# Output projection with channels on partitions, slice logits from its sum, and a gather in two column tiles: a two-layer fused kernel on one Trainium2 core

## The chip, the cores and the metric

The kernel runs on one core of one Trainium2 chip. The metric is the device time of one execution in microseconds (us). A core has five engines that run side by side: TensorE (PE, with its weight loads shown as PEld), VectorE (DVE), ScalarE (ACT), GpSimd (POOL) and SyncE (SP), which here only issues DMAs. They meet at semaphores: an instruction waits until another engine has counted far enough, and everything behind it on its own engine waits with it.

## The reference, cut to what matters

The input is one image of 256 channels and 48 x 48 = 2304 positions ("tokens"). All arithmetic is in fp32.

```python
# layer 0: group norm, attention over all (token, head) pairs, output projection, residual
xt = transpose(group_norm(x))
q, k, v = xt @ Wq.T + bq, xt @ Wk.T + bk, xt @ Wv.T + bv      # 4 heads of 64
A = softmax(qf @ kf.T / 8, axis=1)                            # 9216 x 9216
x = x + (A @ vf).reshape(...) @ Wo.T + bo
# layer 1, attention: tokens are soft-assigned to 64 slices
t = tokens(x); n = layer_norm(t)
h = n @ W0 + b0
sw = softmax(h @ Ws + bs)                                     # 2304 x 64
# q, k, v of the slices: (h @ Wqkv + bqkv) summed over tokens with weights sw,
# divided by the sum of sw; attention among the slices; back to tokens by sw; @ Wout + bout
t = t + slice_attention(...)
# layer 1, experts: top 2 of 8 gates, each expert 256 -> 1024 -> 256 with gelu
t = t + sum of w_e * expert_e(layer_norm(t))
```

## The kernel before

**Stages.** Projections of layer 0; the attention of layer 0; a tail that finishes the last two token tiles; slice attention; gating and routing; the experts. A second copy of the layers for extreme inputs is behind a branch that is not taken.

**Layout.** Tokens are cut into 18 tiles (`NTT`) of 128. `x_sb` holds x with channels on partitions, `[128, 2, 2304]`; `t_sb` holds it with tokens on partitions, 256 channels and 8 columns for gates.

**Projections.** Queries and keys come first, in token blocks; then 18 tiles of values go through the V loop: two matmuls (line 330) into one of five PSUM banks and a VectorE addition into `v_sb` (line 334). Behind it, before the attention, stand fourteen small matmuls (lines 347 to 365) that fold `W0 @ Ws` into the slice weights `Wl` and `Wout @ Wg` into gate columns of `Wout_sb`, with column sums `cs_bc` of the gate weights, by which a mean is taken off later.

**Attention.** The 9216 queries are taken in 18 blocks (`b`), each against 36 pairs of key tiles. A pair is four 64x64-tile matmuls of scores `s`, one exponential `p` on ScalarE over 1024 columns, four matmuls `av` of values, and one VectorE addition into `acc`. `s` has two buffers, `p` five, `av` one. Two blocks make one group `g` of 256 tokens; the normalized result goes to `OT[:, g % 2]`.

**Work between pairs.** In pair 0 of a block, `close` finishes the block before: `both` (the sum of the two halves of `acc`), `partition_all_reduce` of it into `total` on POOL, and `up`, which reads `av`. In pair 1, `between(b - 1)` puts the side work of earlier token tiles on PE, ahead of the first `av` of the block; its VectorE and ScalarE parts go into a list `later`, of which one item is taken per pair, in the order of the ranks that stand beside them. Pieces of side work, each for one token tile `i`:

- `out_proj`: two transposes of `x_sb` and two matmuls with `WoT` in one bank, whose sum is x plus projection with tokens on partitions; `add` puts `bo_bc` to it in `t_sb`, `spread` takes mean and variance and has POOL compute `rstd_t` by a power, `norm` writes `tn`;
- `turn`: two transposes of `tn`, copied to `tnT` by ScalarE;
- `slices`: two matmuls `tnT` x `Wl`; softmax to `sw`, and gate columns of `t_sb`, for which the scale is undone;
- `gather`: two matmuls of 64 columns, `tn` x `sw`, added into `ts_sum`; `sw` is added into `sw_sum`.

`follow(k)` starts `out_proj` of tile k - 2, `turn` of k - 3, `slices` of k - 4 and `gather` of k - 5, two PSUM banks `pa` and `pb` among them:

```python
for lag, (step, ps) in enumerate(
    ((out_proj, pa), (turn, pa), (slices, pb), (gather, pb))
):
    if 0 <= k - 2 - lag < NTT - 2:
        work.extend(step(k - 2 - lag, ps))
```

In the last block, when `later` is empty, `follow` is called up to four more times, so that tiles 0 to 15 are done by its end.

**Order.** `pe`, `dve`, `act` and `pool` are wrappers that keep the program's order; what is issued through `nc.` may be moved by the scheduler (the projections, `nc.vector` constants). DMAs of SP keep their order.

**Tail.** Tiles 16 and 17 need the last two blocks. `out_proj`, `turn` and `slices` run for both, with eight transposes of `sw` and filler matmuls (`busy`, which keep PE occupied) between; then `pts` and `den` take their sums, `ph` is the first matmul of the slice attention. The memory of layer 0 is freed there, and SP loads the expert weights `w2_sb` (8 MB) and `b2_bc` into it.

## Time and profile before

| | us |
|---|---|
| median of 3 runs (lowest to highest) | 1604.61 (1604.38 to 1605.35) |
| the profiled execution, whole | 1603.17 |
| its span, first to last instruction | 1601.5 |
| PE, DVE, ACT, POOL busy in the span | 1571.7, 1059.7, 834.7, 193.2 |
| first score matmul of the attention at | 67.71 |
| last `av` of the attention from | 1224.64 |
| first `ph` of the slice attention at | 1241.68 |
| mean granted TensorE clock | 0.998 |

The profile lists for each engine what ran when. A line of the timeline has the start, the busy time, the engine, the source line (line 60 is that of the wrapper), the operation, `out<-in` by the names of the program, and the number of records merged; in brackets the idle time of the engine before it and what ended that. An fp32 matmul leaves two records, a transpose one. The ends of matmuls are modelled, so their starts are the better measure. The page also has shares by 40 slices, DMA queues, and the chain of work that ended last; that chain goes back only to 1303.9 us, inside the experts, so the attention is read from the timeline.

### The profile page before, as it was taken

Reading aid. Unit: us, or ns where it says so; the run is one execution under the profiler, and the core shown is the slowest. Engines: PE = TensorE matmul, PEld = TensorE weight load, DVE = VectorE, ACT = ScalarE, POOL = GpSimd, SP = SyncE. Lnnn points to the kernel's source line nnn. Section 1 sums busy time; section 2 is a strip of 40 time slices with the busy share of each in tenths; the row PEclk is TensorE's granted clock in tenths of the full one; section 3 lists DMA queues with packets and bytes.
Section 4 is the critical chain, followed back from the end, with each engine's and each line's share of the span. In section 5 each row is a group of like instructions: output and inputs, shape, how many; then the busy total and the mean of one; then the engine's idle time right before and its main releaser. Section 6 shows DMA issues by size and latency. Waiting matters only on the chain. (4 is left out here: it accounts for less than half of the span.)

```text
span 1601.5 us, 32032 instructions
## 1 busy us (share of the span) xinstructions
PE 1571.7 (98%) x13225; PEld 789.6 (49%) x13225; DVE 1059.7 (66%) x1379; ACT 834.7 (52%) x1178; POOL 193.2 (12%) x141
## 2 busy tenths in 40 slices
PE   7999999999999999999999999999999999999997
PEld 3633333333333333333333333333334689999996
DVE  6578788787787877878878778788787721111111
ACT  2266666565665656656656566566564533333331
POOL 0000001011010010110100101101000123433331
PEclk9999999999999999999999999999999999999999
DMA  4000000000000000000000000000001956666664
GB/s 138 1 1 1 1 1 1 1 1 1 1 1 1 2 1 2 1 1 2 1 1 1 1 1 1 1 1 1 1 2 55 300 162 188 180 183 182 181 186 143
DMA packets 38200, 77.58 MB, mean 48 GB/s; under 512 B 3565, under 2 KB 24378, under 8 KB 37914
## 3 DMA queue, kind: packets, MB, share of 16 engines
q1 hardware_dynamic: 30154, 64.78, 12.0%
q0 software_dynamic: 7344, 10.10, 3.7%
q8 instruction: 109, 1.79, 0.5%
q10 hardware_dynamic: 544, 0.52, 0.1%
q14 instruction: 49, 0.40, 0.1%
HBM read 63.07 MB, written 12.32 MB: 47 GB/s over the span
## 5 line engine op out<-in xcount | busy, mean ns | idle before, releaser
L60 ACT ACTIVATE p<-s 128x1024 f32<-128x1024 f32 x648 | 663.8, 1024 | 475.4 <-PE s L60 466.6
L60 DVE TENSOR_TENSOR acc<-acc,p 128x1024 f32<-128x1024 f32 x612 | 748.2, 1222 | 227.5 <-ACT p L60 216.8
L60 PE MATMUL av<-p,v_sb 64*64 64x512 f32 x5184 | 675.7, 590 | 2.1 <-DVE up L60 1.8
L60 PE MATMUL s<-q,kk 64*64 64x512 f32 x5184 | 675.4, 590 | 0.0
L60 PEld LDWEIGHTS s<-q,kk 64*64 64x64 f32 x5184 | 200.9, 133 | 353.2 <-issue 181.3
L60 PEld LDWEIGHTS av<-p,v_sb 64*64 64x64 f32 x5184 | 195.6, 131 | 355.9 <-ACT p L60 200.4
L60 ACT ACTIVATE hid<-ph,bcol 128x128 f32<-128x128 f32 x312 | 89.4, 368 | 200.8 <-PE ph L60 200.1
L60 POOL PARTITION_ALL_REDUCE total<-both x17 | 55.3, 3250 | 962.0 <-DVE both L60 962.0
L60 PE MATMUL py<-w_sb,hid 128*128 x624 | 146.9, 379 | 0.0
L60 PEld LDWEIGHTS ph<-xT,w 128*128 128x128 f32 x1248 | 145.3, 192 | 2.7 <-issue 0.8
L60 PE MATMUL ph<-xT,w 128*128 128x128 f32 x1248 | 145.7, 275 | 0.6 <-issue 0.6
L60 DVE COPY xT<-pt 128x256 f32<-128x256 f32 x39 | 16.5, 424 | 161.0 <-PE pt L60 161.0
L60 PEld LDWEIGHTS py<-w_sb,hid 128*128 128x128 f32 x624 | 112.8, 190 | 12.3
L1133 POOL DMA_INDIRECT t_d<-y,slot_t x38 | 60.1, 1582 | 163.9 <-DVE y L60 146.0
L60 DVE TENSOR_TENSOR y<-py,b_bc 128x256 f32<-128x256 f32 x39 | 16.6, 425 | 77.5 <-PE py L60 77.5
L60 POOL TENSOR_TENSOR rstd_t<-ve,mhalf 128x1 f32<-128x1 f32 (+3 forms) x22 | 28.0, 1273 | 205.2 <-DVE ve L60 205.2
L60 DVE TENSOR_TENSOR acc<-p 128x1024 f32<-128x1024 f32 x18 | 36.4, 2024 | 9.3 <-ACT p L60 9.3
L1133 POOL DMA_INDIRECT xs<-tn_d,slot_t x36 | 38.9, 1080 | 15.8 <-issue 9.9
L60 DVE RECIPROCAL rinv<-rinv 128x256 f32<-128x256 f32 x17 | 29.7, 1746 | 0.0
L318 DVE TENSOR_SCALAR q<-pp,bcol 64x512 f32<-64x512 f32 (+1 forms) x30 | 20.8, 694 | 8.0 <-PE pp L301 7.7
L60 DVE TENSOR_REDUCE up<-av 128x512 f32<-128x1024 f32 x18 | 21.9, 1216 | 0.0
L60 PE MATMUL spin<-Wqkv_sb,ident 128*128 128x256 f32 x90 | 20.9, 381 | 0.0
(292 smaller groups left out, 644.5 us busy)
## 6 DMA issues: line engine op xcount, KB each, us to landing
w<-in_L_ffn_W_dram SPq DMA_DIRECT2D x39, 1024.0 KB, 5.8
w_sb<-in_L_ffn_W_dram SPq DMA_DIRECT2D x8, 1024.0 KB, 11.9
x_sb<-in_x_dram SPq DMA_DIRECT2D x3, 576.0 KB
t_d<-t_sb SPq DMA_DIRECT2D x2, 768.0 KB, 5.4
tn_d<-tn SPq DMA_DIRECT2D x2, 768.0 KB
t_sb<-t_d SPq DMA_DIRECT2D x3, 512.0 KB, 6.2
out_dram<-ob SPq DMA_DIRECT2D x3, 512.0 KB
b_bc<-in_L_ffn_b_dram SPq DMA_DIRECT2D x1, 1024.0 KB
```

The lines of the kernel that those rows point to most:

```text
L60: return self.tc.keep_in_program_order(getattr(self.engine, name)(*args, **kwargs))
L318: nc.vector.tensor_scalar(dst, pq[rows, 0:tn], bcol[rows, B_Q + m : B_Q + m + 1], 0.125, ALU.add, ALU.mult,)
L1133: new = nc.gpsimd.indirect_dma_start(**kwargs)
```

## The change

The side work now goes by groups of two token tiles. `out_proj` computes Wo x O with channels on partitions (four matmuls of 256 columns) and adds it and `bo`, now a column of `bcol`, into `x_sb`. `slices` transposes `x_sb` into one bank for mean, variance and `t_sb`, and multiplies `x_sb` itself with `Wl`, whose columns have had their mean over the 256 channels taken off, so that the mean of a token falls out; the logits are scaled by `rstd_t` afterwards. `turn` and `tnT` are gone, and gate columns need no correction. `gather` has the two tiles of a group in the two column halves of PE: `sw` is the stationary operand (64 columns), `tn` with a column of ones (257) the moving one, and the sums of the halves and of `sw` stay in `sums_of` until the tail folds them with `fold`. `follow` does `out_proj` for even k, `gather` and `slices` for odd k. The last block has two extra calls, not four. In `close`, `up` is taken ahead of `both`. The small matmuls of the weights go into the V loop at tiles 3, 6 and 9. Routing has two operations fewer. The tail does its two tiles as one group.

```diff
-    sw_sum = const.tile([P, S], FP, name="sw_sum")
+    sums_of = const.tile([P, C + 1], FP, name="sums_of")
+    nc.vector.memset(ts_sum[:, 2 * S : 3 * S], 0.0)
+    fold = const.tile([P, 2, S], FP, name="fold")
+    fold_den = const.tile([P, S], FP, name="fold_den")
+    nc.vector.tensor_tensor(fold[:, 1, :], ident[:, 0:S], ident[:, S : 2 * S], ALU.add)
+    nc.vector.tensor_copy(fold[:, 0, :], fold[:, 1, :])
...
+    B_Q, B_K, B_0, B_QK, B_OUT, B_O = 64, 66, 68, 70, 74, 76
...
+        for r, (b, n) in {64: (bq, 2), 66: (bk, 2), 68: (b0, 2), 70: (bqkv, 4), 74: (bout, 2), 76: (bo, 2)}.items():
...
-    bo_bc = load_bcast(bo, C, "bo_bc")
...
+        def slice_weights():
+
+            pw = ps_w.tile([P, 512], FP, name="pw", tag="pw")
+            nc.vector.tensor_copy(Wl[:, :, S : S + E], Wg_sb)
+            for k, b in enumerate((B_0, B_0 + 1, B_OUT, B_OUT + 1)):
+                nc.vector.tensor_copy(brep[:, k, :], bcol[:, b : b + 1].to_broadcast([P, P]))
+            for ci in range(2):
+                for k in range(2):
+                    nc.tensor.matmul(
+                        pw[:, ci * S : (ci + 1) * S], W0T[:, k, ci * P : (ci + 1) * P], Ws_sb[:, k, :],
+                        start=(k == 0), stop=(k == 1),
+                    )
+            for k in range(2):
+                nc.tensor.matmul(
+                    pw[:, 128:192], brep[:, k, :], Ws_sb[:, k, :], start=(k == 0), stop=(k == 1)
+                )
+            nc.vector.tensor_copy(Wl[:, :, 0:S], pw[:, 0:128].rearrange("p (c s) -> p c s", c=2))
+            nc.vector.tensor_tensor(bl_bc, pw[:, 128:192], bs_bc, ALU.add)
+
+        def centred():
+
+            pw = ps_w.tile([P, 512], FP, name="pw", tag="pw")
+            for k in range(2):
+                nc.tensor.matmul(
+                    pw[:, 0 : S + E], ones, Wl[:, k, :], start=(k == 0), stop=(k == 1)
+                )
+            nc.vector.scalar_tensor_tensor(
+                Wl, pw[:, 0 : S + E].unsqueeze(1).to_broadcast([P, 2, S + E]), -1.0 / C, Wl,
+                ALU.mult, ALU.add,
+            )
...
+            elif i == 3:
+                slice_weights()
+            elif i == 6:
+                centred()
+            elif i == 9:
+                gate_weights()
...
+    tn = side.tile([P, 4, C + 1], FP, name="tn")
+    dve.memset(tn[:, :, C : C + 1], 1.0)
+    NG = NTT // 2
...
+    def out_proj(g, ps, _):
+
+        toks = slice(g * TG, (g + 1) * TG)
+        for m in range(2):
+            for c in range(2):
+                pe.matmul(
+                    ps[:, m * TG : (m + 1) * TG], WoT[:, c, m * P : (m + 1) * P], OT[:, g % 2, c, :],
+                    start=(c == 0), stop=(c == 1),
+                )
+
+        def add(m):
+            dve.scalar_tensor_tensor(
+                x_sb[:, m, toks], ps[:, m * TG : (m + 1) * TG], bcol[:, B_O + m : B_O + m + 1],
+                x_sb[:, m, toks], ALU.add, ALU.add,
+            )
+
+        return [(2, lambda: add(0)), (3, lambda: add(1))]
...
+    def slices(g, ps, pl):
+
+        two = range(2 * g, 2 * g + 2)
         for c in range(2):
+            for u, i in enumerate(two):
+                pe.transpose(
+                    ps[:, u * C + c * P : u * C + (c + 1) * P], x_sb[:, c, i * P : (i + 1) * P], ident
+                )
+        for u, i in enumerate(two):
+            at = u * (S + E)
+            for c in range(2):
+                pe.matmul(
+                    pl[:, at : at + P], x_sb[:, c, i * P : (i + 1) * P],
+                    Wl_flat[:, c * (S + E) : c * (S + E) + P], start=(c == 0), stop=(c == 1),
+                )
+        both = pl[:, 0 : 2 * (S + E)].rearrange("p (u s) -> p u s", u=2)
+        lg = small.tile([P, 2, S], FP, name="lg", tag="lg")
+        sm = small.tile([P, 2], FP, name="sm", tag="sm")
+        nm = small.tile([P, 2], FP, name="nm", tag="nm")
+        these = slice(2 * g, 2 * g + 2)
+
+        def keep(u):
+            act.copy(t_sb[:, 2 * g + u, 0:C], ps[:, u * C : (u + 1) * C])
+
+        def spread(u):
             s6 = small.tile([P, 6], FP, name="s6", tag="s6")
+            dve.bn_stats(s6, ps[:, u * C : (u + 1) * C])
+            dve.bn_aggr(stats[:, 2 * g + u, :], s6)
+
+        def scales():
+            ve = small.tile([P, 2], FP, name="ve", tag="ve")
+            dve.tensor_scalar(ve, stats[:, these, 1], 1e-5, None, ALU.add)
+            pool.tensor_tensor(rstd_t[:, these], ve, mhalf[:, 0:2], ALU.pow)
 
         def logits():
+            for u, i in enumerate(two):
+                dve.scalar_tensor_tensor(
+                    lg[:, u, :], both[:, u, 0:S], rstd_t[:, i : i + 1], bl_bc, ALU.mult, ALU.add
+                )
             dve.tensor_reduce(nm, lg, AX.X, ALU.max, negate=True)
 
         def exps():
+            for u in range(2):
+                act.activation(
+                    lg[:, u, :], lg[:, u, :], AF.Exp, bias=nm[:, u : u + 1], accum_out=sm[:, u : u + 1]
+                )
 
         def gates():
+            dve.tensor_copy(t_sb[:, these, C : C + E], both[:, :, S : S + E])
 
         def weights():
             dve.reciprocal(sm, sm)
+            dve.tensor_tensor(sw[:, these, :], lg, bc(sm, [P, 2, S]), ALU.mult)
+
+        def norm(u):
+            i = 2 * g + u
+            dve.tensor_scalar(
+                tn[:, i % 4, 0:C], t_sb[:, i, 0:C], stats[:, i, 0:1], rstd_t[:, i : i + 1],
+                ALU.subtract, ALU.mult,
+            )
+
+        at = 9 if g == NG - 1 else 16
+        return [
+            (2, lambda: spread(0)), (3, lambda: spread(1)), (4, lambda: keep(0)), (5, lambda: keep(1)),
+            (6, scales), (8, logits), (9, exps), (10, gates), (11, weights),
+            (at, lambda: norm(0)), (at, lambda: norm(1)),
+        ]
+
+    def gather(g, _, pl):
+
+        new = pl[:, 200 : 200 + C + 1]
+        for u in range(2):
+            i = 2 * g + u
             pe.matmul(
+                new[u * S : (u + 1) * S, :], sw[:, i, :], tn[:, i % 4, :], start=True, stop=True
             )
 
         def add():
+            if g == 0:
+                dve.tensor_copy(sums_of, new)
             else:
+                dve.tensor_tensor(sums_of, sums_of, new, ALU.add)
+            if g == NG - 2:
+                dve.tensor_scalar(fold_den, fold[:, 1, :], sums_of[:, C : C + 1], None, ALU.mult)
+
+        return [(1, add)]
...
+                up = at_1.tile([P, QB], FP, name="up", tag="up")
+
+                def halved():
+                    dve.tensor_add(both, st["acc"][:, 0, :], st["acc"][:, 1, :])
+
+                if last:
+                    halved()
+                dve.tensor_reduce(up, st["av"].rearrange("p r q -> p q r"), AX.X, ALU.add)
                 if not last:
+                    halved()
...
-                for lag, (step, ps) in enumerate(
-                    ((out_proj, pa), (turn, pa), (slices, pb), (gather, pb))
-                ):
-                    if 0 <= k - 2 - lag < NTT - 2:
-                        work.extend(step(k - 2 - lag, ps))
+                steps_of = ((gather, k // 2 - 2), (slices, k // 2 - 1)) if k % 2 else ((out_proj, k // 2 - 1),)
+                for step, g in steps_of:
+                    if 0 <= g < NG - 1:
+                        work.extend(step(g, pa, pb))
...
-                work, pa, pb = follow(b if b < NQB - 1 else NQB + 3)
+                work, pa, pb = follow(b if b < NQB - 1 else 2 * NQB)
...
-                    elif b == NQB - 1 and pair < NPAIR - 1 and drained < 4:
-
-                        work, _, _ = follow(NQB - 1 + drained)
+                    elif b == NQB - 1 and pair < NPAIR - 1 and drained < 2:
+
+                        work, _, _ = follow(NQB - 1 + 2 * drained)
...
+    last = NG - 1
+    pa = ps_o.tile([P, 512], FP, name="pm", tag="pm")
+    for w in in_turn(out_proj(last, pa, None)):
+        w()
+    weights_transposed(0, 4)
+    weights_transposed(4, 4)
+    pe.matmul(den, ones, fold_den, start=True, stop=False)
+    for c in range(2):
+        pe.matmul(
+            pts[:, c, :], sums_of[:, c * P : (c + 1) * P], fold.rearrange("p a s -> p (a s)"),
+            start=(c == 0), stop=False,
+        )
+    busy(1, spin)
+    pa, pb = (ps_o.tile([P, 512], FP, name="pm", tag="pm") for _ in range(2))
+    for w in in_turn(slices(last, pa, pb)):
+        w()
+    busy(2, spin)
     for c in range(2):
         for i in range(NTT - 2, NTT):
             pe.matmul(
-                pts[:, c, :], tn[:, i % 6, c * P : (c + 1) * P],
+                pts[:, c, :], tn[:, i % 4, c * P : (c + 1) * P],
                 sw[:, i - 1 : i + 1, :].rearrange("p i s -> p (i s)"),
-                start=(i == NTT - 2), stop=(i == NTT - 1),
+                start=False, stop=(c == 1 and i == NTT - 1),
...
-            dve.tensor_tensor(
-                ts_sum[:, 0 : 2 * S].rearrange("p (c s) -> p c s", c=2),
-                ts_sum[:, 0 : 2 * S].rearrange("p (c s) -> p c s", c=2), pts[:, :, S : 2 * S], ALU.add,
+            dve.tensor_copy(
+                ts_sum[:, 0 : 2 * S].rearrange("p (c s) -> p c s", c=2), pts[:, :, S : 2 * S]
             )
...
-        dve.tensor_tensor(
-            lg, bc(stats[:, :, 0], full), cs_bc.unsqueeze(1).to_broadcast(full), ALU.mult
-        )
-        dve.tensor_tensor(lg, t_sb[:, :, C : C + E], lg, ALU.subtract)
-        dve.tensor_tensor(lg, lg, bc(rstd_t, full), ALU.mult)
+        dve.tensor_tensor(lg, t_sb[:, :, C : C + E], bc(rstd_t, full), ALU.mult)
         dve.tensor_tensor(lg, lg, bg_bc.unsqueeze(1).to_broadcast(full), ALU.add)
```

The functions `gate_weights` (the last six of the fourteen matmuls, at tile 9) and the removed bodies are left out; the removed ones stand with the kernel above.

## The prediction

> **What bounds the kernel now.** I read the page's busy shares first, then the timeline of TensorE, then where TensorE pauses. The shares:

> ```profile
> PE 1571.7 (98%) x13225; PEld 789.6 (49%) x13225; DVE 1059.7 (66%) x1379; ACT 834.7 (52%) x1178; POOL 193.2 (12%) x141
> ```

> TensorE (PE) is never idle for long, so a microsecond removed from its queue counts unless something else comes late. The timeline of PE at the start of block 7 of the attention (18 blocks of 36 key pairs) shows the unit of work and the "side work" between two pairs:

> ```profile
> 512.74 1.04 PE L60 MATMUL s<-q,kk 64*64 64x512 f32 x8
> 513.71 0.44 PE L60 MATMUL pa<-ident,x_sb 128*128 128x128 f32 x2
> 513.98 1.03 PE L60 MATMUL pa<-WoT,OT 128*128 128x256 f32 x4
> 514.85 0.38 PE L60 MATMUL pa<-ident,tn 128*128 128x128 f32 x2
> 515.06 0.61 PE L60 MATMUL pb<-Wl,tnT 128*128 128x128 f32 x4
> 515.51 0.56 PE L60 MATMUL pb<-sw,tn 128*128 128x64 f32 x4
> 516.00 1.09 PE L60 MATMUL av<-p,v_sb 64*64 64x512 f32 x8
> 516.91 1.04 PE L60 MATMUL s<-q,kk 64*64 64x512 f32 x8
> ```

> Columns: start, busy time, engine, line, instruction, count; an fp32 matmul leaves two records, a transpose one. Starts tell more than the overlapping durations: a pair (s and av, eight matmuls) takes 1.717 us from s to s everywhere else in the block, here it takes 516.91 - 512.74 = 4.17, so the side work costs 2.45 us of pure PE time. Differences of starts give its parts: two transposes 0.22 (0.11 each), two 256-column matmuls 0.87 (0.435 each), two transposes 0.21, two 128-column matmuls 0.45 (0.223 each), two 64-column ones 0.39, and about 0.31 of transitions: 0.11 ahead of the first, 0.05 in it, 0.10 after the last, 0.05 in the first av.

> Blocks 1 and 2 have no side work, and there PE waits for `up`:

> ```profile
> 132.11 0.69 DVE L60 TENSOR_TENSOR both<-acc 128x512 f32<-128x512 f32 x1
> 132.12 1.04 PE L60 MATMUL s<-q,kk 64*64 64x512 f32 x8
> 132.72 1.22 DVE L60 TENSOR_REDUCE up<-av 128x512 f32<-128x1024 f32 x1
> 134.08 1.09 PE L60 MATMUL av<-p,v_sb 64*64 64x512 f32 x8 [0.92 <-DVE up L60]
> ```

> Summed over the timeline, in excess of 1.717 a pair: blocks 1 and 2 cost 1.12 and 1.14, block 3 (projection only) 1.40, block 4 1.61, block 5 2.06, blocks 6 to 17 2.45 each (29.4); block 17 drains the rest at four more places, 2.46, 1.65, 1.35 and 0.90. Total **43.1 us**. This is what the change works on.

> [...] the four quadrant matmuls of 512 columns take 0.86 together. [...] for 256 columns [...] the trace has 0.435. So 257 columns are an estimated 0.44.

> **The change, part by part.**

> 1. *Attention boundaries.* Even k (the argument of `follow`) now gets only the projection of two token tiles: four 256-column matmuls, 4 x 0.435 = 1.74, + 0.31 = 2.05. Odd k gets the gather of an earlier group and the slices: four transposes 0.44, four 128-column matmuls 0.89, + 0.31 = 1.64 without gather. The gather is two 257-column matmuls in the two column halves. Where 128x64 tiles were used before:

> ```profile
> 1226.71 0.65 PE L60 MATMUL pb<-both,ones 128*64 128x256 f32 x4 [0.99 <-DVE both L60]
> 1227.30 3.29 PE L60 MATMUL pa<-Wqkv_sb,ident 128*128 128x256 f32 x14
> ```

> two such matmuls take 0.59 to the next start, not 2 x 0.435: they run side by side[...]. So the gather is 0.44 + 0.15 and an odd boundary 2.23. Bounds: 2.08[...] to 2.67 (halves one after the other).
> The four `tn` transposes of two tiles (0.43) and the half-empty 64-column gathers are what disappears.
> After: blocks 1 and 2, 2w; k = 2, 4 to 14, 7 x 2.05 = 14.35; k = 3, 1.64; k = 5 to 15, 6 x 2.23 = 13.38; block 17: 2.05, then one drain of gather and slices 2.23, then the last gather alone, 0.31 + 0.59 + 0.25 for the `tn` issued just ahead of it (that wait is 0.2 to 0.3 in the same place today) = 1.15.
> w: `up` now goes ahead of `both`. It must still wait for the last av (issue ends 132.12; VectorE follows a PE issue end by 0.2 in the V loop), so it starts at 132.32 instead of 132.72, and w = 1.12 - 0.40 = 0.72. `both` and the all-reduce behind it slip by some 0.8: POOL's 3.25 us then end at 137.0, and `sides` reads them at 138.9, so this is covered; in later blocks `sides` comes later still.
> Sum 1.44 + 14.35 + 1.64 + 13.38 + 2.05 + 2.23 + 1.15 = 36.2, a gain of **6.9 us**. Side work of 1.64 or more covers w.

> 2. *What the new work puts on other engines.* ACT has 0.69 us free a pair. Two `keep` copies (0.37 each, a pair apart) fit. The two exponentials come together: 2 x (0.35 + 0.19) = 1.08, overlapping by some 0.1 to 0.2, so p is late by 0.2 to 0.4 once per odd block. PE takes p's product 0.39 after p is ready, so I charge 0 to 0.1 x 8, **+0.3**. DVE has 0.49 free a pair; its steps are 0.6 (spread), 0.75 (logits), 0.45 (weights), 0.41 (norms, add). With five p buffers it may fall some three pairs behind, as it does today in the 1.75 us reciprocal. Cost 0.

> 3. *Slice weights in the V loop.* The fourteen small matmuls ahead of the attention (64.60 to 67.62) move into the V loop: same count, same PE time. But they were the cover for the last `v_sb` addition:

> ```profile
> 49.92 14.84 PE L330 MATMUL pp<-WvT,t_sb 128*128 128x256 f32 x68
> 64.80 0.42 DVE L334 TENSOR_TENSOR v_sb<-pp,bv_bc 128x256 f32<-128x256 f32 x1 [0.44 <-PE pp L330]
> 67.71 3.07 PE L60 MATMUL s<-q,kk 64*64 64x512 f32 x16
> ```

> In the built program the first s matmul waits for that addition (its bank is taken over). It ends 0.62 after the last V matmul's issue, with the signal some 0.68. The cover gone, PE stalls: **+0.6** (0.45 if part of today's slow first s hides in it, to 0.7). The copies into `brep` and `Wl` stand early in DVE's order, and V's own additions leave DVE 0.44 idle a tile, so the moved matmuls find their inputs.

> 4. *Start.* `fold` puts two 64-column VectorE instructions between the group-norm statistics, which DVE does without a gap from 4.72 to 11.18 ahead of everything: **+0.25** (0 to 0.35). The row of `bo` is one more small DMA on SP ahead of Wv and Wo (0.25 to 0.5 us of its queue); Wv lands near 13.2 and is used at 23.25. Covered; without the cover 0.5.

> 5. *Tail, last two tiles.* Today:

> ```profile
> 1239.58 0.25 DVE L60 TENSOR_SCALAR sw<-lg,sm 128x64 f32<-128x64 f32 x1
> 1241.68 1.16 PE L60 MATMUL ph<-ts_sum,W_sb 128*128 128x128 f32 x8 [0.35 <-ACT swT L60]
> ```

> After: projection from 1230.64, four matmuls to 1232.4; then PE's written order holds eight transposes (0.87), the folded sums (0.2 + 0.45) and a filler (0.44), so the slices' transposes start near 1234.4 although `x_sb` is ready at 1233.4; transposes and slices to 1235.7. Spread of both from 1235.0, `ve` 1236.25, POOL's two-column power 0.87 (the 128x2 one at 1266.28) to 1237.3, logits to 1238.05, exponentials to 1239.0, weights to 1239.6. The four pts matmuls then end near 1240.55, as now. One turn, three gate operations and the sum disappear, but the two tiles now go through in step. **0** (-0.6 to +0.8).

> 6. *w2 prefetch and routing.* The first w2 load on SP waits for the last reader of `x_sb`: now the slices' matmul (1235.9) instead of the projection (1233.1), 2.8 us later for all eight loads and b2 on that queue. SP then issues t_d's first rows near 1258.3 instead of 1257.9; tn_d's rows wait for ACT at 1268.8 anyway, and rows are first fetched at 1290. Cost 0; uncovered, 2.8. The two routing operations that go were done while VectorE waited for POOL's `rstd_t` until 1267.19: gain 0.

> Sum: -6.9 + 0.3 + 0.6 + 0.25 = **-5.75 us** on the profiled execution's 1603.17 (span 1601.5 and 1.67 around it): 1597.4. The median of the runs, 1604.61, lies 1.44 above that execution, so I forecast 1604.61 - 5.8 = **1598.8**.

> **Rivals.** (a) *The column halves run one after the other*: +0.44 x 8 = 3.5, time 1602.3. Against it stands the 0.59 above; for it, that both halves go to one PSUM bank, as those also did. Chance 0.06. (b) *The later w2 loads show*: DMA runs near 350 to 370 GB/s from 1241 to 1265, so the delay is not caught up; time 1601.6. Against it: no instruction there waits for a load. Chance 0.06. (c) *Slower*: DVE is in order, and `logits` waits for POOL's power, which takes 1.50 in the attention for one column. At 1.6 times that for two, 2.4 us, it delays the sums by 0.9, within the p buffers. Only beyond some 6 us would ACT find no buffer and PE stop; at 7.5 each of eight groups loses 1.5, +12, time 1610.8. Chance 0.04. (d) *More gain*: [...] the tail in the lower half of its bounds: 1597. It is in the range of the forecast.

> **Numbers.** Forecast 0.84 (its own range 1596.2 to 1601.0), (a) 0.06, (b) 0.06, (c) 0.04. A measurement here can tell about 0.2%, 3.2 us, from no change: faster means below 1601.4. The range 1596.0 to 1601.6 takes in the bounds of terms 1 to 5, and (b). Faster 0.86, same 0.10, slower 0.04.

> **What would show it.** Step 1: pairs still at 1.717, boundaries alternating near 2.05 and 2.2, the two `pb<-tn,sw` matmuls starting together. Step 3: first s behind the V loop by 0.6 with DVE `v_sb` as releaser. Step 5: `ph<-ts_sum` as far behind the last av as today (17.0). Wrong, if odd boundaries exceed 2.7 or pairs inside blocks exceed 1.717, or if the expert phase starts later relative to `ph<-ts_sum`.

## The result and the profile after

The changed kernel takes 1595.95 us (median of 6 runs, 1592.28 to 1596.63), the kernel before on the same chip 1604.22 (6 runs, 1601.78 to 1605.35): ratio 0.9946, 95% interval 0.9933 to 0.9959. It is faster, as forecast, but by 8.3 us instead of 5.8, so the time lies just below the range (1596.0 to 1601.6). The six executions of the changed kernel and the five of after_again below fall into two groups by their mean granted clock: eight with 0.997 took 1595.3 to 1596.6 us, three with 0.999 or 1.000 took 1592.3 to 1593.3. The first profile, which the lines below show, is one of the three.

The shares of the page: all four engines that the change touches have less to do than before, ScalarE and POOL hardly less.

```profile
PE 1562.8 (98%) x13157; PEld 778.2 (49%) x13157; DVE 1029.8 (65%) x1276; ACT 833.8 (52%) x1178; POOL 192.2 (12%) x132
```

TensorE's timeline at the first boundary with the projection alone and at the first with gather and slices (start, busy time, engine, line, instruction, count):

```profile
256.37 1.05 PE L60 MATMUL s<-q,kk 64*64 64x512 f32 x8
257.35 1.99 PE L60 MATMUL pa<-OT,WoT 128*128 128x256 f32 x8
259.28 1.09 PE L60 MATMUL av<-p,v_sb 64*64 64x512 f32 x8
260.19 1.04 PE L60 MATMUL s<-q,kk 64*64 64x512 f32 x8
...
447.60 1.04 PE L60 MATMUL s<-q,kk 64*64 64x512 f32 x8
448.56 0.65 PE L60 MATMUL pb<-tn,sw 128*64 128x257 f32 x4
449.15 0.65 PE L60 MATMUL pa<-ident,x_sb 128*128 128x128 f32 x4
449.64 1.06 PE L60 MATMUL pb<-Wl,x_sb 128*128 128x128 f32 x8
450.63 1.09 PE L60 MATMUL av<-p,v_sb 64*64 64x512 f32 x8
451.54 1.04 PE L60 MATMUL s<-q,kk 64*64 64x512 f32 x8
```

From s to s: 260.19 - 256.37 - 1.717 = 2.10 for the projection, 451.54 - 447.60 - 1.717 = 2.22 for gather and slices; forecast 2.05 and 2.23. The gather's two products take 0.59 to the next start. Where the rest of the time came from, in us by stages, in two profiles of each kernel (the second ones are the runs before_again and after_again below):

| stage | before | again | after | again | forecast change |
|---|---|---|---|---|---|
| to the first s | 67.71 | 67.55 | 67.82 | 68.83 | +0.85 |
| first two pairs, over 1.717 each | 0.89 | 0.89 | -0.17 | -0.16 | 0 |
| rest of the attention, to the last av | 1156.03 | 1156.04 | 1149.40 | 1149.39 | -6.6 |
| last av to `ph<-ts_sum` | 17.05 | 17.06 | 16.76 | 17.82 | 0 |
| to the first expert product | 53.40 | 53.86 | 53.62 | 54.64 | 0 |
| to the last expert tile | 276.85 | 277.89 | 276.44 | 275.79 | 0 |
| to the end of the span | 29.52 | 28.85 | 27.66 | 27.64 | 0 |
| span | 1601.46 | 1602.14 | 1591.52 | 1593.95 | |

The attention gave what was forecast, 6.6 us. Three stages moved that the forecast had at zero: the first pairs (-1.06), the tail (-0.29 and +0.76), and the end (-1.86 and -1.21), which the diff does not touch. (In before_again half the clock, from 1296.48 to 1299.89, also fell into the first expert tile; the 1.0 us by which its 277.89 exceeds 276.85 fit this.)

The start of the attention after, on TensorE, with what ended its waits in brackets:

```profile
65.63 1.67 PE L385 MATMUL pp<-WvT,t_sb 128*128 128x256 f32 x7
67.82 1.95 PE L60 MATMUL s<-q,kk 64*64 64x512 f32 x16 [0.52 <-DVE tn L60]
70.18 1.09 PE L60 MATMUL av<-p,v_sb 64*64 64x512 f32 x8 [0.41 <-ACT p L60]
```

The stall of step 3 is there, 0.52. But the first av comes 2.36 after the first s; before, it came 70.54 - 67.71 = 2.83 after, with no wait shown. Why the profile says itself, in the granted clock. The next lines have a stretch of time, its length, the busy time of PE, PEld, DVE, ACT and POOL in it (with instructions), the granted clock, and two columns for DMA; first the kernel before, then the kernel after:

```profile
64.99:68.40 3.41, 3.41 (x34) 3.06 (x37) 0.81 (x6) 0.00 (x0) 0.00 (x0) 1.00 0.02 5
68.40:71.81 3.41, 3.41 (x20) 1.00 (x16) 0.07 (x1) 2.00 (x2) 0.00 (x0) 0.50 0.00 0
71.81:75.22 3.41, 3.41 (x36) 1.22 (x32) 2.25 (x2) 1.43 (x3) 0.00 (x0) 1.00 0.00 0
```

```profile
64.99:68.40 3.41, 2.89 (x19) 2.01 (x21) 1.48 (x5) 0.00 (x0) 0.00 (x0) 1.00 0.00 0
68.40:71.81 3.41, 3.00 (x32) 0.87 (x28) 0.73 (x1) 1.94 (x2) 0.00 (x0) 1.00 0.00 0
71.81:75.22 3.41, 3.41 (x36) 1.21 (x32) 1.97 (x3) 2.05 (x2) 0.00 (x0) 1.00 0.00 0
```

Before, TensorE had half its clock from 68.40 to 71.81, for 3.41 us at the entry to the attention; after, it had all of it.

### The profile page after: what moved, and what is told of

Its sections match the earlier page's. It is cut to its first block, busy times and chain, and to the rows that moved or that the text cites. A ratio compares the mean times of both kernels' runs of the same rounds, so it can differ in the third digit from the quotient of the medians.

```text
span 1591.5 us, 31789 instructions
## 1 busy us (share of the span) xinstructions
PE 1562.8 (98%) x13157; PEld 778.2 (49%) x13157; DVE 1029.8 (65%) x1276; ACT 833.8 (52%) x1178; POOL 192.2 (12%) x132
## 5 line engine op out<-in xcount | busy, mean ns | idle before, releaser
L60 DVE TENSOR_TENSOR acc<-acc,p 128x1024 f32<-128x1024 f32 x612 | 749.2, 1224 | 251.3 <-ACT p L60 245.7
L60 ACT ACTIVATE p<-s 128x1024 f32<-128x1024 f32 x648 | 663.4, 1024 | 468.8 <-PE s L60 464.7
L60 PE MATMUL av<-p,v_sb 64*64 64x512 f32 x5184 | 675.1, 590 | 1.8 <-DVE up L60 1.2
L60 PE MATMUL s<-q,kk 64*64 64x512 f32 x5184 | 674.1, 589 | 0.5 <-DVE tn L60 0.5
L60 PEld LDWEIGHTS s<-q,kk 64*64 64x64 f32 x5184 | 200.8, 133 | 354.9 <-issue 181.9
L60 PEld LDWEIGHTS av<-p,v_sb 64*64 64x64 f32 x5184 | 194.6, 131 | 358.1 <-ACT p L60 202.3
L60 ACT ACTIVATE hid<-ph,bcol 128x128 f32<-128x128 f32 x312 | 89.5, 368 | 200.2 <-PE ph L60 199.4
L60 POOL PARTITION_ALL_REDUCE total<-both x17 | 71.2, 4187 | 989.0 <-ACT p L60 810.6
L60 PE MATMUL py<-w_sb,hid 128*128 x624 | 146.9, 379 | 0.0
L60 PEld LDWEIGHTS ph<-xT,w 128*128 128x128 f32 x1248 | 145.2, 192 | 3.4 <-issue 1.6
L60 PE MATMUL ph<-xT,w 128*128 128x128 f32 x1248 | 145.8, 275 | 1.0 <-issue 0.6
L60 DVE COPY xT<-pt 128x256 f32<-128x256 f32 x39 | 16.5, 424 | 161.6 <-PE pt L60 161.6
L60 PEld LDWEIGHTS py<-w_sb,hid 128*128 128x128 f32 x624 | 112.8, 190 | 12.3
L60 DVE TENSOR_TENSOR y<-py,b_bc 128x256 f32<-128x256 f32 x39 | 16.6, 425 | 77.5 <-PE py L60 77.5
L1163 POOL DMA_INDIRECT xs<-tn_d,slot_t x36 | 38.9, 1080 | 15.7 <-issue 10.1
L60 POOL TENSOR_TENSOR rstd_t<-ve,mhalf 128x2 f32<-128x2 f32 (+2 forms) x13 | 11.1, 852 | 171.1 <-DVE ve L60 171.1
L60 DVE RECIPROCAL rinv<-rinv 128x256 f32<-128x256 f32 x17 | 29.7, 1746 | 0.0
L60 DVE TENSOR_REDUCE up<-av 128x512 f32<-128x1024 f32 x18 | 22.0, 1224 | 5.0 <-PE av L60 5.0
L60 DVE TENSOR_TENSOR acc<-p 128x1024 f32<-128x1024 f32 x18 | 22.1, 1226 | 4.9 <-ACT p L60 3.3
L60 PE MATMUL spin<-Wqkv_sb,ident 128*128 128x256 f32 x86 | 20.0, 381 | 0.0
```

Source lines behind the costliest of these rows:

```text
L60: return self.tc.keep_in_program_order(getattr(self.engine, name)(*args, **kwargs))
L1163: new = nc.gpsimd.indirect_dma_start(**kwargs)
```

## The experiments

Two theories stood for each of the unexpected gains: that it belongs to the change (or to something in it that could be had alone), and that it is chance. Each run was compared with the kernel before on its own chip.

**before_again and after_again**, both kernels unchanged.

> The kernel before, unchanged, for a second profile and for the scatter of its time. In the first profile the sixteen s products at 67.7 us and the first av products ran at half pace (0.85 us between groups of four where later ones take 0.43) and the granted clock of 68.8 to 70.8 us was 0.50. Theory A (it follows from 3.1 us of narrow products, 8 and 64 columns, just ahead): the half pace shows again, and the first two pairs of attention together cost about 0.9 us over the steady 1.72 us per pair. Theory B (chance, once in some executions): here they cost about 0, as in the changed kernel's profile (-0.17). Ratio 1.000 in both. The last output store's issue on ACT's queue, 2.52 us in the first profile against 0.83 after the change: if it is scatter, it differs here.

> The changed kernel as it is, for a second profile and a ratio in the same company: 0.995. The store issue 0.6 to 0.8 us; no half clock at the start of attention; the tail 16.8 us, or some 0.8 to 1.4 us more where half the clock falls into it (two of its four variants so far: 17.56 and 18.13 us), which its 2.65 us wait for the slice weights allows.

Ratios 0.9998 (0.9990 to 1.0007) and 0.9948 (0.9934 to 0.9961). The stages are in the table. The half clock came back in before_again, the slow store too (2.47 us); after_again had neither, but half the clock in its tail, after a wait that the kernel before has only half as long:

```profile
1229.11 1.03 PE L60 MATMUL spin<-Wqkv_sb,ident 128*128 128x256 f32 x4
1232.79 1.77 PE L60 MATMUL pts<-sw,tn 128*128 128x128 f32 x8 [2.65 <-DVE sw L60]
1234.36 0.95 PE L60 MATMUL den<-sw,ones 128*128 128x64 f32 x4
```

In the first profile of the changed kernel the pts products took 1.00 to the next start (1231.78 to 1232.78), here 1.57. The clock around the wait, in after_again and then in the first profile:

```profile
1229.74:1233.15 3.41, 0.76 (x5) 0.36 (x4) 2.01 (x9) 1.15 (x6) 0.69 (x1) 1.00 0.66 208
1233.15:1239.98 6.83, 6.48 (x28) 5.77 (x27) 2.58 (x9) 0.27 (x1) 0.00 (x0) 0.50 1.07 347
```

```profile
1227.65:1231.06 3.41, 1.48 (x10) 1.03 (x8) 2.46 (x11) 1.27 (x6) 0.70 (x1) 1.00 0.36 88
1231.06:1234.47 3.41, 2.33 (x19) 2.14 (x20) 1.82 (x7) 0.41 (x3) 0.00 (x0) 1.00 1.02 348
```

**weights_inside**, the kernel before with this part of the change alone; **weights_behind**, the changed kernel without it; **gate_last**, with a third of it undone.

```diff
 # weights_behind (gate_last: the last call only); weights_inside does the reverse to the kernel before
-            elif i == 3: slice_weights()
-            elif i == 6: centred()
-            elif i == 9: gate_weights()
+        slice_weights(); centred(); gate_weights()      # behind the V loop
```

> The kernel before with only its slice and gate weights' products moved into the V loop, in three parts behind tiles 3, 6 and 9. Theory A: the first s waits about 0.5 us for the last V tile, the half pace at the start of attention is gone (fill -0.2 instead of +0.9): together -0.5 to -0.6 us, ratio 0.9996. Theory B, the prediction's own term: the wait alone is added, +0.5 to +0.6 us, ratio 1.0004. The profile of the first 75 us tells them apart; the ratio hardly can.

> The changed kernel with slice_weights, centred and gate_weights called behind the V loop instead of within it. Each needs the one before through DVE, so some 1.5 us of PE waits show between them, and the first s no longer waits 0.52 us for the last V tile. Theory A (narrow products and gaps ahead of attention cost TensorE half its clock for a window of some 3.4 us): granted clock near 0.5 for a stretch at the start of attention, pair fill back at about +0.9 instead of -0.17, about 2.0 us slower than the changed kernel: some 1598 us, ratio to before 0.996. Theory B (the fill was chance): the clock stays 1.00, about 1.0 us slower than the changed kernel, some 1597.

> The changed kernel with gate_weights alone behind the V loop: 1.25 us of products of 8 columns between the last V tile and the first s. Theory A: [...] the clock stays 1.00 and the 0.52 us wait of the first s is covered: 0.5 us faster than the changed kernel, ratio to before about 0.9943. If any narrow work at that place costs the clock, the fill goes back to +0.9 and the kernel is 0.5 us slower than the changed one, ratio about 0.995.

weights_inside: 0.9998 (0.9989 to 1.0006); first V product to first s 20.22 us instead of 19.53 (+0.69, the stall with it), first pairs -0.17 instead of +0.89, clock 1.00. weights_behind: 0.9954 (0.9940 to 0.9968), and against theory A the clock stayed 1.00, first pairs -0.17. gate_last: 0.9937 (0.9924 to 0.9951), the first s without a wait, 19.53, first pairs -0.17. So products of few columns ahead of the attention do not always cost the clock; one profile of each kernel could not tell chance from cause.

**clock_probe** measured the disputed cost by itself, many times over in one run.

> Nothing of the reference is computed: 96 stretches, each of 24 products of 128x256 (10 us, as the V loop), then one of six kinds of work, then 12 score-like products of 512 columns on quarters of the array, 16 stretches of each kind in turn. The kinds: 28 passes of 64 and 8 columns in the order of the kernel before (about 3.1 us); 28 passes of 8 columns; 28 passes of 64 columns; 12 passes of 8 columns (1.3 us); about 3 us in which TensorE waits for VectorE; and the products of weights_behind with their two waits. Theory A (a stretch of about 3 us in which few columns pass costs half the clock for the next 3.4 us): score products at half pace after most stretches of the first two kinds and of the wait, hardly after the 1.3 us kind, and after 64 columns less than after 8. Theory A2 (waits don't count, only narrow products do): none after the wait. Theory B (chance that has nothing to do with what ran before): the same share after each kind.

Three neighbouring stretches in the timeline: behind 8-column products the 24 score passes (s) take 42.18 to 47.51, behind as many of 64 columns 61.42 to 64.16.

```profile
38.67 3.58 PE L60 MATMUL thin<-W,x_sb 128*128 128x8 f32 x28
42.18 5.40 PE L60 MATMUL s<-x_sb 64*64 64x512 f32 x24
47.51 10.91 PE L60 MATMUL wide<-W,x_sb 128*128 128x256 f32 x48
58.26 3.23 PE L60 MATMUL thin<-W,x_sb 128*128 128x64 f32 x28
61.42 2.81 PE L60 MATMUL s<-x_sb 64*64 64x512 f32 x24
```

The clock around another stretch of 8-column products (s from 143.60; these lines have no column for ACT):

```profile
140.28:143.70 3.42, 3.42 (x34) 3.37 (x36) 0.00 (x0) 0.00 (x0) 1.00 0.02 5
143.70:147.11 3.41, 3.41 (x20) 1.03 (x24) 0.00 (x0) 0.00 (x0) 0.50 0.00 0
147.11:150.52 3.41, 3.41 (x24) 2.31 (x17) 0.00 (x0) 0.00 (x0) 1.00 0.00 0
```

| what ran between (16 times each) | s slow | s, us (2.74 at full clock) |
|---|---|---|
| as before the change, 3.1 us of 64 and 8 columns | 5 | 4.28 to 4.34 |
| 8 columns only, 3.1 us | 11 | 4.42 to 5.33 |
| 64 columns only, 3.2 us | 0 | |
| 8 columns, 1.3 us | 0 | |
| 2.2 us waiting for VectorE, one 8-column product | 11 | 4.40 to 4.43 |
| as in weights_behind, 4.3 us with two waits | 5 | 5.16 to 5.22 |

Theory A holds, and what looks like a lottery follows a grid. In this trace the granted clock is either 1.00 or 0.50. Apart from one that the end of the program cuts off, it has 32 stretches of half clock, 21 of 3.41 us and 11 of 6.83 us, and each begins a whole number of 3.41 us after the others; the program has no such period. The 16 repeats of a kind fall, in turn, on three places of that grid, and each place gives the same answer every time. So the counts stand for one or two places of three, and each zero for three places without half clock. In this run half the clock followed 8-column products, or the wait, where more than 2.5 us of them lay between two neighbouring grid points; where a point divided them so that 2.2 us or less lay on either side, it did not. 1.3 us of 8 columns and 3.2 us of 64 columns had none at the three places that they fell on. What sets the grid is not shown.

The kernels fit the same grid. The small products lay almost wholly in one step of it in the kernel before (64.60 to 67.71, step 64.99 to 68.40) and in before_again (64.43 to 67.55, step 64.27 to 67.68), and the next step ran at half clock. In before_act1 below a grid point, 66.41, falls amid them (65.25 to 68.36), and the clock stayed 1.00; the point is counted back in steps of 3.413 from its half stretch at 1295.22 (in before_again the two half stretches begin at 67.68 and 1296.48, which is 360 such steps). The first s of weights_behind comes 0.39 of a step behind a grid point; in the probe its products kept the clock at 0.41 to 0.43 and at 0.60, and lost it only at 0.52 to 0.56.

**before_act1 and act_less1** moved one thing: the place of the last-but-one output store in ScalarE's instruction stream.

```diff
 # before_act1, to the kernel before
     make_identity(nc, ident)
+    nc.scalar.copy(extra, ident[:, 0:1])
 # act_less1, to the changed kernel: WoutT's eviction
-            nc.scalar.copy(dst, pw)
+            nc.vector.tensor_copy(dst, pw)
```

> The kernel before with one more instruction on ScalarE, a copy of one column at the very start, where ScalarE idles. In three profiles of kernels whose ScalarE has the kernel before's number of instructions the first output store on its queue took 2.47 to 2.53 us to issue, in three of kernels with one more 0.62 to 0.83, and the last part of the program (from the last 32 ph to the end) 28.9 to 29.6 us against 27.5 to 28.0. Theory: where that store stands in ScalarE's instruction stream decides it: here it takes 0.6 to 0.9 us, and the kernel is 1.6 us faster than before, ratio 0.9990. Rival: it belongs to what the change does in the data or the other queues: 2.5 us again, ratio 1.0000.

> The changed kernel with one copy less on ScalarE: WoutT's eviction in the V loop goes to VectorE, which has room there. The output store on ScalarE's queue goes from the 2356th to the 2355th place of that engine's instructions, where it stood in the kernel before. Theory (the place decides): the store's issue takes 2.5 us again instead of 0.6 to 0.8, and the last part of the program is 1.5 to 2.5 us longer: 1.5 to 2.5 us slower than the changed kernel, ratio to before about 0.996. Rival: something else that the change did shortened the end: 0.8 us, no slower, ratio 0.9946.

ScalarE's timeline around that store, in the order before, before_act1, after, act_less1 (each with the copy ahead of it):

```profile
1592.21 0.37 ACT L60 COPY ob<-ph 128x256 f32<-128x256 f32 x1 [1.29 <-PE ph L60]
1592.62 2.52 ACTq L60 DMA_DIRECT2D out_dram<-ob  x1
```

```profile
1592.37 0.37 ACT L60 COPY ob<-ph 128x256 f32<-128x256 f32 x1 [1.01 <-PE ph L60]
1592.77 0.74 ACTq L60 DMA_DIRECT2D out_dram<-ob  x1
```

```profile
1584.69 0.37 ACT L60 COPY ob<-ph 128x256 f32<-128x256 f32 x1 [1.00 <-PE ph L60]
1585.10 0.83 ACTq L60 DMA_DIRECT2D out_dram<-ob  x1
```

```profile
1584.53 0.37 ACT L60 COPY ob<-ph 128x256 f32<-128x256 f32 x1 [1.28 <-PE ph L60]
1584.94 3.10 ACTq L60 DMA_DIRECT2D out_dram<-ob  x1
```

One idle copy more takes the store's issue from 2.52 to 0.74 us, and the kernel to 0.9982 (0.9974 to 0.9990); one less takes it from 0.83 to 3.10, and the ratio from 0.9948 to 0.9973 (0.9963 to 0.9983). The last stage was 26.35 and 30.66 us. The last store stands behind this one on the same queue, so the end of the program moves with it: from the copy ahead of the store to the end of the span it is 9.25 and 8.84 us in the two profiles of the kernel before and 9.42 in act_less1, but 6.68 in before_act1 and 6.83 and 6.86 in the changed kernel. The place is worth 2.2 to 2.6 us. The theory holds in both directions, and in all thirteen profiles of these kernels: 2.47 to 3.10 us for the issue in the four with the kernel before's number of ScalarE instructions, 0.59 to 0.83 in the nine with one more. Of the 2.9 us that before_act1 gained, a part is the clock: 8 of its 14 executions have a mean clock of 0.999 or more, of the kernel before's on the same chip 1 of 21. The change has one ScalarE instruction more ahead of the store (the traces record 2278 instead of 2277) and got this by luck.

**gather_serial**, both tiles of a gather in one half of the array.

```diff
-                new[u * S : (u + 1) * S, :], sw[:, i, :], tn[:, i % 4, :], start=True, stop=True
+                new[0:S, :], sw[:, i, :], tn[:, i % 4, :], start=(u == 0), stop=(u == 1)
```

> The changed kernel with both tiles of a gather in one column tile: the second product adds to the first in rows 0 to 63. The same sum. Theory (the two halves of the array ran side by side): each of the seven gathers' boundaries takes 0.43 us more than its 2.22, +3.0 us together, ratio to before about 0.9965. Rival: the halves took turns anyway, no difference to the changed kernel, ratio 0.9946.

```profile
448.72 1.08 PE L60 MATMUL pb<-tn,sw 128*64 128x257 f32 x4
449.73 0.44 PE L60 MATMUL pa<-ident,x_sb 128*128 128x128 f32 x2
```

1.01 to the next start instead of 0.59; the boundary takes 2.65 instead of 2.22, as expected, and the attention 3.15 us more. Ratio 0.9972 (0.9961 to 0.9982). Half the clock fell into its tail besides (18.13 us), and all eight of its executions have a mean clock of 0.997 or 0.998; this fits the whole differing by 3.9 us rather than 3.0.

**both_first**, the order in `close` as before.

> The changed kernel with the sum of acc ahead of the reduction of av in close, as before. VectorE's first acc<-p of each block takes 2.0 us again instead of 1.23, as POOL's sum over partitions starts earlier and runs beside it; POOL's sum 3.25 us instead of 4.19. Theory (VectorE has 35% of slack and neither is awaited at once): the boundaries stay at 31.2 us in all but the last block and the time does not move, ratio 0.995. Rival: the late acc holds up a pair: 0.3 us in each of 16 blocks, 5 us, ratio 0.998.

The groups by shape, first the changed kernel, then both_first (count, busy, mean ns of one):

```profile
L60 POOL PARTITION_ALL_REDUCE total<-both x17 | 71.2, 4187 | 989.0 <-ACT p L60 810.6 <-DVE both L60 118.5 <-ACT low L60 60.0
L60 DVE TENSOR_TENSOR acc<-p 128x1024 f32<-128x1024 f32 x18 | 22.1, 1226 | 4.9 <-ACT p L60 3.3
```

```profile
L60 POOL PARTITION_ALL_REDUCE total<-both x17 | 55.1, 3241 | 987.7 <-DVE both L60 987.7
L60 DVE TENSOR_TENSOR acc<-p 128x1024 f32<-128x1024 f32 x18 | 36.6, 2033 | 9.1 <-ACT p L60 9.1
```

VectorE and POOL changed as expected. The ratio, 0.9947 (0.9933 to 0.9960), cannot tell it from the changed kernel, but the trace can: blocks 1 and 2 cost 1.12 and 1.14 instead of 0.78 and 0.80, all later ones the same. The order is worth 0.68 us and only there; this is the gain that step 1 forecast as w.

**best and best_dve2**, a version faster than both; best_dve2 moves VectorE's later instructions two places on.

```diff
 # best = gate_last, and in the tail:
     weights_transposed(0, 4)
+    # slices of the last two tiles come here, ahead of:
     weights_transposed(4, 4)
     ...
-    busy(1, spin)
-    # slices, then
-    busy(2, spin)
+    busy(5, spin)
```

> The changed kernel with gate_weights behind the V loop, and in the tail the last two tiles' slices ahead of the second half of the slice weights' transposes and of the sums' products, with five filler products where TensorE waited 2.65 us. The first s comes 0.5 to 0.7 us earlier; the tail from the last av to the slice attention takes 15.9 us instead of 16.76, and its chance of half the clock falls. Together 1.4 to 1.6 us faster than the changed kernel, ratio to before about 0.9935. Rival: the tail is bound by VectorE's chain from the additions to the slice weights, which starts no earlier: only the 0.5 us, ratio 0.994.

> The kernel of the run best with tn's memset in three instructions instead of one, which puts VectorE's later work two places on. In the changed kernel, its repeat and best the second or a near load of t_sb at the end took 1.1 to 1.6 us to issue on SyncE instead of 0.43 and the second ob came 9.6 to 10.1 us after the last ph began; in the kernel before with one more ScalarE instruction, and in act_less1, no load was slow and it came at 8.8 to 8.9. Theory (places in the other engines' streams move this stall too; gather_serial, with two more on VectorE, was at 9.14): ob at 8.8 to 9.2, the end 0.8 to 1.1 us shorter, ratio to before about 0.992. Rival (SyncE's own place decides, which is the same in all): 1.1 us stay, ratio 0.9926.

best: 1591.39 us (5 runs), ratio 0.9926 (0.9912 to 0.9939), against 0.9946 and 0.9948 of the changed kernel, whose intervals overlap it slightly. TensorE's tail:

```profile
1228.01 2.32 PE L60 MATMUL spin<-Wqkv_sb,ident 128*128 128x256 f32 x10
1230.59 1.16 PE L60 MATMUL pts<-sw,tn 128*128 128x128 f32 x8 [0.25 <-DVE sw L60]
```

The wait of 2.65 us is 0.25, the tail 15.75 us in the profiles of both kernels, and the stretch from the last av to the first expert product 69.1, where the changed kernel had 70.4 and 72.5. All ten executions of best and best_dve2 have a mean clock of 0.999 or more (1590.1 to 1592.1 us). Against the three of the changed kernel with such a clock (1592.3 to 1593.3) that is some 1.5 us; the rest of the gain fits the half clock that its tail no longer draws. best_dve2: 0.9922 (0.9909 to 0.9936), no different: its second t_sb load still took 1.33 us to issue on SyncE. The rival's time held, but its reason is not shown: with the same instructions on SyncE no load was slow in before_act1 and act_less1. (In after_again the slow load was the third, with 0.87 us, less than the expectation says.)

## Why the prediction was right and wrong

- **Step 1 and 2, boundaries and exponentials: right.** 6.63 us against 6.9 - 0.3. Even boundaries 2.09 (forecast 2.05), odd 2.22 (2.23), k = 3 1.64 (1.64), blocks 1 and 2 0.79 (0.72). gather_serial shows that side by side was the right reading of the 0.59 (1.01 with both in one half); what takes the 0.15 in it beyond the estimated 0.44 of one product is not shown. That the total agrees to 0.1 us is in part luck: the 0.3 for late exponentials does not show (the pairs within blocks add nothing to 1.717), and the even boundaries, which took a little more each, use up about as much.
- **Step 3, the lost cover: the stall right, the other side of it missed.** V loop to first s grew by 0.69 (forecast 0.6). But the step counted the moved products as "same count, same PE time", and did not ask why the first s of the kernel before was slow, though it named that slowness ("part of today's slow first s"). It was the half clock, 1.06 us in two of three profiles of kernels with these products there (before_act1 was spared it). On an average execution that is less than 1.06.
- **Step 4, start: neither shown nor refuted.** The first projection product began at 15.57, 15.96 and, in before_act1, 15.45 us before, at 15.72 and 15.62 after; this scatter is larger than the 0.25 that was forecast.
- **Step 5, tail: right at full clock (-0.29 for 0), but its chance was not seen.** The step let the two tiles go "in step" and did not say what TensorE does meanwhile, though its own times leave TensorE some 3 us (slices done at 1235.7, slice weights at 1239.6, two fillers between). TensorE waits 2.65 us instead of 1.35. Seven profiles have this tail. In four of them (after_again, weights_behind, gate_last, gather_serial) half the clock followed for 3.41 or 6.83 us, and the stretch to the first expert product took 71.5 to 72.8 us; in the other three (the first profile, act_less1, both_first) it did not, and the stretch took 70.1 to 70.7. The grid shows in the lines under after_again: there the wait (1230.14 to 1232.79) lies within one step, in the first profile the point 1231.06 divides it. weights_behind does not fit by its wait alone, for a point divides that too. The eight executions of eleven with a mean clock of 0.997 say that the typical one pays; its price, some 3 us, is more than step 3's other side gained. Where in those without a profile the half clock fell is not shown.
- **Step 6, w2 loads: right.** The first w2 load was issued 11.3 us after the last av instead of 8.5, and the first expert product came 53.3 to 53.9 us after `ph<-ts_sum` in kernels with and without the change, where no half clock fell between.
- **The sum: the failed step.** It held every stage behind the w2 loads at zero, because the diff does not touch them. The end took 1.2 to 1.9 us less, through the place of one store in ScalarE's stream. Beside it, step 3's +0.6 left out the half clock that the move took away (up to 1.06 us less), and step 5's zero erred the other way (some 3 us in eight executions of eleven). With the place of the store alike, before_act1 against the changed kernel, the ratios are 0.9982 and 0.9948: 5.5 us by their middles (with their intervals some 2.5 us either way), where the sum had 5.75. So close a match is in part luck, since the two kernels pay for the half clock at different places and not equally often. The end kept only 1.2 to 1.9 of the 2.2 to 2.6 us that the place is worth: in the changed kernel the second copy into `ob` began 11.6 us after the last expert tile instead of 10.5. In the first profile the second t_sb load took 1.60 us to issue on SyncE instead of 0.43, in after_again the third 0.87. What decides that is open: SyncE's own instructions are the same in all, and act_less1 was free of it.
- **Rivals.** (a), serial halves, fell with 0.59. (b), late w2 loads, did not show. (c), VectorE waiting for POOL, did not happen: POOL's power for two columns took 0.74 us on average. (d), 1597, was nearest in time but not in its reasons.

What was not tried: an explanation of why that one place is slow; no run here shows its cause.

## What to carry to other kernels

Price products of few columns and waits of TensorE not only by their time: in clock_probe half the clock, for 3.41 or 6.83 us, followed 3.1 us of 8-column products in 11 of 16 stretches and a wait of 2.2 us with one such product in 11 of 16 (1.7 to 2.6 us more for the scores behind them). So spread them among wide products, as weights_inside does (clock 1.00 there), or fill a wait with wide ones, as best does (wait 0.25 instead of 2.65 us, mean clock 0.999 or more). Look at the mean clock of every execution before taking one profile for the typical one. Before crediting a change with a time, look at the stages that it doesn't touch; where the end moves, add or remove one idle instruction on the queue that ends last and measure again. And profile twice: on these kernels two executions differ by 4 to 5 us, and the profiles show where.
